# A Mamba, attention and expert kernel on one core: activation table, convolution taps, wide weights and PSUM halves

## The chip, the cores and the metric

The kernel runs on one core of a Trainium2 chip, as a single program. The metric is the device time of one execution in microseconds (us); the number given for a kernel is the median of several executions. Engines are written as in the profile: PE is TensorE (its weight loads PEld), DVE is VectorE, ACT is ScalarE, POOL is GpSimd, SP is the SyncE queue that issues nearly all transfers.

## The reference, cut to what matters

The input x is 4 images of 128 channels and 64 x 64 points, so 4096 tokens each. All is float32.

```python
# layer 0: x + L0(groupnorm(x))
gf   = mamba(tok(x), 2 heads, state 16) + tok(x)          # the "seed": 8 channels
seed = x + detok(gf)
xs   = layernorm(x) split into 8 lanes of 16 channels
ys   = mamba(mamba(xs, state 64), state 64) + xs * skip   # the "cascade", 4 heads, chunks of 64
out  = layernorm(ys + mix(mean(ys))) + seed
h    = dwconv3x3(out @ fc1)                               # 256 channels, 9 taps each
out  = out + gelu(h + dw_b) @ fc2                         # the FFN
# one Mamba: in a chunk of 64, with Acs the running sum of dt * A
Y    = (C @ B^T * tril(exp(Acs_l - Acs_s))) @ x  +  C @ state * exp(Acs)
# layer 1
t = t + softmax(q k^T / sqrt(32)) v @ Wo                  # 4 heads of 32, 4096 keys
t = t + top-2 of 8 experts, weighted by softmax of the router
```

## The kernel before

**Layer 0** works on blocks of 512 tokens (`LB`), eight per image. The list `items` holds 8 seed blocks and 64 cascade blocks (4 images, 8 blocks, 2 Mambas); each goes through four stages, and one step of the loop in `layer0` records the back stage of one item, the front of the next, the preparation of the one after it and the outer part of a fourth, side by side. All these operations go to a recorder, `Deck`. `Deck.flush` then runs a list schedule over them: it has a price for each operation (`price`, with `SIDE` for small matmuls), a rank from the program's order with offsets (`BEHIND`), and rings, which count a tile's buffers. What comes out is one fixed order per engine. It is issued by one line, so in the profile almost all of layer 0 has the line L991, and rows are told apart by their tiles.

The names in `back`: `exponentials` has PE write the exponents ps_d of one pair of chunks (index u, four per block) and ACT take e = exp(ps_d), 128 x 1024. `weigh` multiplies e by the masked products gm on DVE. `within` has PE multiply e with the inputs xp into the PSUM tile py (two banks, 256 columns used of each), and DVE adds its four pieces to y. The items py, e and y above are these.

ACT holds one table of functions at a time. `flush` puts a load of the table with both exponential and logarithm ahead of an exponential or logarithm that follows a SiLU or a GELU; loads for SiLU and GELU, and for whatever else finds its function missing, are put in when the program is compiled.

**The FFN** of an image (`ffn`) runs over its 8 blocks: `merge` (layer norm, seed, residual), `conv` (expand by fc1 to two halves of 128 channels, kept in two fixed tiles h with a halo, then nine taps per half as DVE instructions into acc), `close` (GELU, fc2, residual, store). Three images' FFNs are recorded along with the Mamba steps. The fourth has no Mamba work left beside it: it is recorded into a second flush, with `early`, the first image's projections to q, k and v for the attention (`prepare` in `projections`).

**Layer 1** (`layer1`) is in an order written by hand. A unit is one image, one block of 512 queries and one head: 128 units of 8 groups. A group (`scores`, `context`) has four row-shift matmuls (L1772) and four score matmuls (L1778) into two PSUM tiles ps_s, two exponentials on ACT (L1782) that read them into e, sums of e on POOL (L1784, L1786), four matmuls of e with v (L1799), and four matmuls (L1740) with a DVE maximum each (L1742) for a later unit. L1772 of a group needs the exponentials of the group before to have read its tile. In between, small steps of `prepare` (the next image's projections), `tail` (output projection, router, experts) and `shift` are paid from a budget. Steps with a logarithm are the inverse roots in `rsqrt` (L1029, L1030), the ones in `prepare` (L1480, L1482) and the softmax's denominator in `tail` (L1597, L1598). The layer begins with this line, ahead of the statement that fixes the order of its engines:

```python
        nc.scalar.preload_act_table_set(LNEXP)      # L1577
        ctx.enter_context(tc.manual_schedule(engines={ENG.PE, ENG.DVE, ENG.Pool, ENG.Activation}))
```

Of the kernel before, what the change touches and what calls it, by code (L numbers as in the profile page):

```python
# [31 lines left out]
LB = 512  # L32
# [243 lines left out]
class Mamba:  # L276
# [344 lines left out]
    def back(self, it, out):  # L621
        sh, s, nc = self.sh, self.s, self.sh.nc
        work, const, ng = sh.work, sh.const, s.ng
        y, zs = it["y"], it["zs"]
        y4 = y.rearrange("p (u g c l) -> p u g c l", u=NU, g=ng, c=2)
        es = {}

        def exponentials(u):
            rt = it["rt"]
            ds = [sh.wide("ps_d") for _ in range(2)]  # L630
            for j2 in range(2):
                for g in range(ng):
                    for j in (2 * j2, 2 * j2 + 1):
                        rows = slice(32 * j, 32 * j + 32)
                        dv = ds[j2][:, j % 2, 0:256 * ng].rearrange("s (h g l) -> s h g l", h=4, g=ng)
                        for c in range(2):
                            nc.tensor.matmul(dv[:, :, g, :], lhsT=sh.lt[rows, g, u, Q * c:Q * c + 128],
                                             rhs=rt[rows, :, u, c, :], start=c == 0, stop=c == 1)
            es[u] = []
            for k in range(2):  # L640
                e = work.tile([128, 2, 4, ng * Q], F32, tag="e", bufs=E_BUFS, name="e")
                nc.scalar.activation(e.rearrange("s j h x -> s j (h x)"), ds[k][:, :, 0:256 * ng], AF.Exp)
                es[u].append(e)

        def weigh(u):
            U, i = divmod(u, 2)
            for k, e in enumerate(es[u]):
                for jj in range(2):

                    nc.vector.scalar_tensor_tensor(  # L650
                        e[:, jj], e[:, jj], 1.0,
                        it["gm"][U][:, 2 * i + k, jj:jj + 1, :].to_broadcast([128, 4, ng * Q]), ALU.min, ALU.mult)

        def within(u):
            U, i = divmod(u, 2)
            py = sh.psy.tile([128, 2, LB], F32, tag="y", name="py")
            pyv = py[:, :, 0:128 * ng].rearrange("p c (h x) -> p c h x", h=2)
            for k, e in enumerate(es.pop(u)):
                for g in range(ng):
                    for f in range(2):  # L660
                        for jj in range(2):
                            j = 2 * k + jj
                            for c in range(2):
                                rows = slice(64 * c, 64 * c + 64)
                                nc.tensor.matmul(pyv[32 * j:32 * j + 32, c, :, Q * g:Q * g + Q],
                                                 lhsT=it["xp"][U][rows, g, 4 * i + j, 16 * f:16 * f + 32],
                                                 rhs=e[rows, jj, 2 * f:2 * f + 2, Q * g:Q * g + Q],
                                                 start=f == 0, stop=f == 1)
            for f, name in enumerate(("even", "odd")):
                for c in range(2):  # L670
                    nc.vector.scalar_tensor_tensor(y4[:, u, :, c, :], pyv[:, c, f, :].rearrange("p (g l) -> p g l", g=ng),
                                                   const(name), y4[:, u, :, c, :], ALU.mult, ALU.add)

        exponentials(0)
        yield
        exponentials(1)
        weigh(0)
        yield
        for u in range(NU):
            within(u)  # L680
            if u + 1 < NU:
                weigh(u + 1)
            if u + 2 < NU:
                exponentials(u + 2)
            yield


        nc.gpsimd.tensor_mul(zs, y, zs)
        yield
        yield  # L690
        nc.scalar.activation(y, zs, AF.Square)
        yield

        def by_token(t):
            return t.rearrange("p (u g c l) -> p g c u l", u=NU, g=ng, c=2)

        def product(name, lhsT, rhs):
            p = sh.ps(name)
            for g in range(ng):
                nc.tensor.matmul(p.rearrange("p (c u l) -> p c u l", c=2, l=Q), lhsT=lhsT[:, g, :], rhs=rhs[:, g],  # L700
                                 start=g == 0, stop=g == ng - 1)
            return p

        pm = product("ps_ms", self.ms, by_token(y))
        r = y[:, 0:LB]
        nc.scalar.activation(r, pm, AF.Ln, bias=sh.eps, scale=4.0 / s.nh)
        yield
        nc.scalar.activation(r, r, AF.Exp, scale=-0.5)
        yield
        yield  # L710
        out(product("ps_out", self.wo, by_token(zs)), r)
        yield
# [35 lines left out]
class Op:  # L748
# [3 lines left out]
    def __init__(self, engine):  # L752
        self.engine, self.calls, self.cost, self.deps, self.users = engine, [], 0.0, set(), []
        self.ready, self.rank, self.uses, self.set, self.phase = 0.0, 0.0, set(), None, None
        self.out = self.src = None
        self.both = False
# [4 lines left out]
SIDE = {"py": 0.030, "ps_yo": 0.0215, "ps_d": 0.07}  # L761


class Deck:


    def __init__(self, nc):
        self.nc, self.ops, self.seen, self.rings, self.ring_of = nc, [], {}, {}, {}
        self.phase, self.stage, self.held = None, None, set()
        self.make, self.made, self.count = {}, {}, 0  # L770
# [27 lines left out]
    def record(self, engine, name, args, kw):  # L798
# [4 lines left out]
        src = ins[-1].tensor.name if engine == "tensor" and ins else None  # L803
        op = self.ops[-1] if self.ops else None
        gelu = AF.Gelu_apprx_tanh in args
        if not (op is not None and op.engine == engine and (
                engine == "tensor" and op.out == out.tensor.name and op.src == src or gelu and op.set == GELU)):
            op = Op(engine)
            op.out, op.src = out.tensor.name, src
# [5 lines left out]
        for kind, ap in aps:  # L815
# [10 lines left out]
            if tile in self.ring_of:  # L826
                op.uses.add(tile)
# [3 lines left out]
    def price(self, engine, name, args, kw, out, ins, op):  # L831
# [4 lines left out]
        if engine == "tensor":  # L836
            tile = out.tensor.name.rsplit("_", 1)[0]
# [25 lines left out]
        return 0.15 + (0.00052 if quick else 0.00104) * (free(ins[0]) if name == "tensor_reduce" else n)  # L863
# [12 lines left out]
    def flush(self, tc):  # L876
# [16 lines left out]
        for i, op in enumerate(ops):  # L893
            op.rank = -i - self.BEHIND.get((op.stage, op.engine), 0)
        room, head = dict(self.rings), {}
        phases, whole = {}, {}
        for op in ops:
            if op.set == SILU:
                phases[op.phase] = phases.get(op.phase, 0) + 1
                whole.setdefault(op.phase, set()).update({op.out} & op.uses)  # L900
# [9 lines left out]
        while events:  # L910
# [16 lines left out]
            for e in engines:  # L927
# [3 lines left out]
                while ready[e]:  # L931
# [8 lines left out]
                    for t in whole[op.phase] - opening if op.set == SILU and lock is None else opens:  # L940
# [22 lines left out]
                for t in op.uses - opening:  # L963
# [21 lines left out]
        for i in order:  # L985
# [4 lines left out]
            for name, args, kw in op.calls:  # L990
                getattr(getattr(self.nc, op.engine), name)(  # L991
                    *[self.real(a) for a in args], **{k: self.real(a) for k, a in kw.items()})
        self.ops, self.seen = [], {}
# [12 lines left out]
class Ring:  # L1006
# [5 lines left out]
    def tile(self, shape, dtype, tag=None, bufs=None, name=None):  # L1012
# [10 lines left out]
        return t.ap()  # L1023

# [56 lines left out]
def layer0(tc, T, td, const, ident, eps, where, batches, qkv):  # L1081
# [9 lines left out]
    with ExitStack() as ctx:  # L1091
# [60 lines left out]
        sh.psy = ring(scan, "psy", 1, space=PSUM)  # L1152
        gfd = dram.tile([128, L], F32, name="gfd")

        def load(b, k):
# [128 lines left out]
        def ffn(b):  # L1284

            outs, accs = {}, {}
# [12 lines left out]
            def merge(k):  # L1299

                y = work.tile([128, LB], F32, tag="outs", bufs=3, name="outs")
# [12 lines left out]
                xg = load(b, k)  # L1314
# [13 lines left out]
            def conv(k):  # L1328

                w1 = P("fc1").rearrange("p (g o) -> p g o", g=2)  # L1330
                accs[k] = []
                for g in range(2):
# [18 lines left out]
                    acc = work.tile([128, LB], F32, tag="acc", name="acc")  # L1351
                    a3 = acc.rearrange("p (r w) -> p r w", w=IMG)
                    for i in range(9):
                        tap = h[:, i // 3:i // 3 + 8, i % 3:i % 3 + IMG]
                        w = P("dw")[:, 9 * g + i:9 * g + i + 1]
                        if i == 0:
                            nc.vector.tensor_scalar(a3, tap, w, P("dw_b")[:, g:g + 1], ALU.mult, ALU.add)
                        else:
                            nc.vector.scalar_tensor_tensor(a3, tap, w, a3, ALU.mult, ALU.add)
# [4 lines left out]
            def close(k):  # L1364

                acc = accs.pop(k)
                for a in acc:
                    nc.scalar.activation(a, a, AF.Gelu_apprx_tanh)
                nc.scalar.preload_act_table_set(LNEXP)
                xin = load(b, k)  # L1370
# [11 lines left out]
            for k in range(NBLK + 2):  # L1382
                if k < NBLK:
                    yield from merge(k)
                if k > 1:
# [14 lines left out]
        for s in range(-2, len(items) + 1):  # L1400
# [12 lines left out]
            if 0 < s and items[s - 1].last:  # L1413
                if pending is not None:
                    run((pending, FFN))
                pending = deck.staged("ffn", ffn(items[s - 1].b))
        deck.flush(tc)
        scan.close()
        pw, pp = ring(ctx, "first", 2), ring(ctx, "psf", 4, space=PSUM)
# [3 lines left out]
                              lambda name: pp.tile([128, LB], F32, tag="m", name=name), qkv)  # L1423
# [9 lines left out]
        run((pending, FFN), (early(), 5 * NBLK + 7))  # L1433
# [20 lines left out]
def projections(nc, td, const, eps, P, work, ps, qkv):  # L1454
# [9 lines left out]
    def prepare(b, k):  # L1464
# [19 lines left out]
        nc.gpsimd.tensor_mul(xl, xl, r)  # L1484
# [4 lines left out]
        nc.gpsimd.tensor_mul(v, v, f)  # L1489
        yield 0.4, False  # L1490
        rsqrt(nc, v, v, eps6)
        nc.gpsimd.tensor_add(tk, tk, xl)
        nc.sync.dma_start(out=td[b, :, blk(k)], in_=tk)
        yield 0.4, False
        nc.gpsimd.tensor_mul(v, v, xl)
# [3 lines left out]
        def lower(f, hi, dst):  # L1499
            lo = tmp("lo", "lo", 2, F32R)  # L1500
            nc.gpsimd.tensor_sub(lo, f, hi.bitcast(F32))
# [34 lines left out]
def layer1(tc, T, td, const, ident, eps, where, out, batches, qkv):  # L1536
# [15 lines left out]
    with ExitStack() as ctx:  # L1552
# [27 lines left out]
        prepare = projections(nc, td, const, eps, P, work, ps, qkv)  # L1580
# [355 lines left out]
```

## Time and profile before

| what | value |
|---|---|
| median of 3 executions | 8652.13 us (8643.69 to 8671.25) |
| profiled execution | 8631.42 us, span 8629.6 us |
| granted PE clock, mean | 0.952 |
| busy, share of the span | PE 90%, DVE 74%, ACT 62%, POOL 56% |
| Mamba layer, 100 to 3600 us | PE 3011, DVE 2655, ACT 2499, POOL 466 us busy |
| last FFN with early projections, 3600 to 3860 us | PE 143, DVE 187, ACT 115, POOL 84 us busy |
| attention and experts, 3910 to 8570 us | PE 4498, DVE 3449, ACT 2732, POOL 4248 us busy |

A row of the groups gives line, engine, operation, tiles (out<-in), shapes and count, then the busy time and the mean duration in ns of one instruction, then the engine's idle time just before them with what ended it. A row of the waits gives who waited for whom: total us, times, longest. A row of a timeline gives start, duration, engine, line, operation and tiles, with the idle time before it in brackets. PEclk is the share of its full clock that PE was granted. An fp32 matmul appears as two records.

### The profile page before, as it was taken

The page shows a single profiled execution, that of the slowest core. Times are in us where ns is not written, and L with a number is a line of the kernel's source. Part 1 is how long each engine was busy: PE and PEld are TensorE (multiplying, and loading weights), DVE is VectorE, ACT ScalarE, POOL GpSimd, SP SyncE. Part 2 cuts the span into 40 slices and gives each one's busy share as a digit, 9 for nine tenths or more (in the row PEclk, how much of TensorE's full clock was granted, in tenths as well). Part 3 has the DMA queues.
Part 4 walks back from the last instruction along what each step waited for, and adds up shares of the span by engine and source line. Part 5 has one row for each costly group of instructions (what it writes and reads, how often), then busy time and mean ns, then how long its engine had stood idle before and what let it go on. Part 6 is the DMA issues. An engine that isn't in the chain of part 4 may idle for free.

```text
span 8629.6 us, 191814 instructions
## 1 busy us (share of the span) xinstructions
PE 7746.4 (90%) x80156; PEld 4572.8 (53%) x80156; DVE 6391.4 (74%) x11795; ACT 5390.8 (62%) x6666; POOL 4824.7 (56%) x3273
## 2 busy tenths in 40 slices
PE   5888888888888888759999999999999999999998
PEld 3566666666666666424454545545444545455544
DVE  5767677877887787767777777777777777777775
ACT  5776677777777677535656556565556565555554
POOL 1111111111111111138999899998889998999997
PEclk9999999999999999869999999999999999999999
DMA  4211211211112111135444445444444544444442
GB/s 136 88 45 46 56 40 47 60 51 50 52 55 59 54 52 46 50 107 131 121 127 116 127 112 135 120 122 123 121 117 123 128 120 127 115 113 118 120 117 61
DMA packets 306609, 800.58 MB, mean 93 GB/s; under 512 B 43984, under 2 KB 61008, under 8 KB 288848
## 3 DMA queue, kind: packets, MB, share of 16 engines
q1 hardware_dynamic: 304848, 780.94, 34.3%
q8 instruction: 633, 10.37, 0.5%
q10 hardware_dynamic: 432, 5.12, 0.2%
q14 instruction: 232, 1.90, 0.1%
q0 software_dynamic: 464, 2.25, 0.1%
HBM read 595.19 MB, written 192.94 MB: 91 GB/s over the span
## 4 chain that ended last, share of the span: by engine, by line
PE 39%; POOL 14%; ACT 6%; DVE 5%; issue 3%; DMA 1%; SPq 0%; POOLq 0%; ACTq 0%; DVEq 0%
POOL s L1784 9%; PE ps_mx L1740 8%; PE acc L1799 7%; PE ps_s L1778 6%; POOL es L1786 4%; PE ps_s L1772 3%; ACT e L1782 2%; PE ps_den L1812 2%; PE ps_e L1688 2%; PE py L991 1%; DVE mx L1742 1%; DVE acc L991 1%; PE ps_d L991 1%; PE ps_ms L991 1%; PE ps_x L991 1%
## 5 line engine op out<-in xcount | busy, mean ns | idle before, releaser
L1742 DVE TENSOR_REDUCE mx<-ps_mx 128x1 f32<-128x512 f32 x4096 | 2791.9, 689 | 951.7 <-PE ps_mx L1740 944.1
L1782 ACT ACTIVATE e<-ps_s 128x1024 f32<-128x1024 f32 x2048 | 1985.3, 1021 | 1633.2 <-PE ps_s L1778 1533.9
L1784 POOL TENSOR_TENSOR s<-e 128x1024 f32<-128x1024 f32 x1024 | 2441.5, 2384 | 338.2 <-ACT e L1782 334.6
L1740 PE MATMUL ps_mx<-k,q 128*128 128x512 f32 x4096 | 1892.6, 472 | 63.9 <-DVE mx L1742 29.7
L1786 POOL TENSOR_TENSOR es<-s 128x512 f32<-128x512 f32 x1024 | 1311.7, 1281 | 80.3
L1778 PE MATMUL ps_s<-q,k 128*128 128x512 f32 x4096 | 1291.4, 397 | 0.0
L1799 PE MATMUL acc<-e,V 128*32 128x512 f32 x8192 | 1100.1, 609 | 0.0
L1740 PEld LDWEIGHTS ps_mx<-k,q 128*128 128x128 f32 x4096 | 780.4, 191 | 545.0 <-DVE mx L1742 215.9
L1778 PEld LDWEIGHTS ps_s<-q,k 128*128 128x128 f32 x4096 | 779.2, 190 | 138.6 <-issue 2.9
L991 DVE SCALAR_TENSOR_TENSOR e<-e,gm 128x512 f32<-128x512 f32 (+1 forms) x1152 | 718.4, 666 | 82.4 <-ACT e L991 82.2
L1772 PEld LDWEIGHTS ps_s<-mr,ones 32*128 32x128 f32 x4096 | 215.2, 182 | 990.8 <-ACT e L1782 587.6
L991 DVE SCALAR_TENSOR_TENSOR y<-py,const,y 128x128 f32<-128x128 f32 (+1 forms) x1152 | 367.8, 339 | 462.5 <-PE py L991 461.4
L1772 PE MATMUL ps_s<-mr,ones 32*128 32x512 f32 x4096 | 571.8, 497 | 92.2 <-ACT e L1782 91.2
L991 ACT ACTIVATE e<-ps_d 128x1024 f32<-128x1024 f32 (+1 forms) x576 | 550.5, 976 | 165.8 <-PE ps_d L991 151.5
L991 PE MATMUL py<-e,xp 64*32 64x128 f32 x17408 | 518.0, 276 | 44.7 <-DVE y L991 43.8
L991 POOL TENSOR_TENSOR zs<-y,zs 128x1024 f32<-128x1024 f32 (+1 forms) x72 | 173.7, 2412 | 563.5 <-DVE y L991 563.0
L991 POOL TENSOR_TENSOR u<-acs 128x512 f32<-128x512 f32 x72 | 76.1, 1057 | 737.5 <-DVE acs L991 643.5
L991 PEld LDWEIGHTS py<-e,xp 64*32 64x32 f32 x17408 | 400.5, 107 | 139.5 <-issue 66.6
L991 PE MATMUL ps_d<-rt,lt 32*128 32x256 f32 x4352 | 374.2, 309 | 29.3 <-ACT e L991 13.0
L991 DVE SCALAR_TENSOR_TENSOR acc<-h,pb,acc 128x512 f32<-128x512 f32 x512 | 385.6, 787 | 3.8
L991 POOL CAST x<-halo_casc 128x8 fp32r<-128x8 f32 x64 | 18.6, 291 | 636.0 <-PE ps_C L991 635.9
L991 PEld LDWEIGHTS ps_d<-rt,lt 32*128 32x128 f32 x4352 | 270.3, 188 | 186.3 <-issue 72.2
(351 smaller groups left out, 12266.3 us busy)
## 6 DMA issues: line engine op xcount, KB each, us to landing
k<-kd SPq DMA_DIRECT2D x512, 512.0 KB, 6.3
x<-hl SPq DMA_DIRECT2D x256, 256.0 KB, 5.2
V<-vd SPq DMA_DIRECT2D x128, 512.0 KB, 10.2
cd<-raw SPq DMA_DIRECT2D x256, 256.0 KB, 5.1
parts<-cd SPq DMA_DIRECT2D x128, 512.0 KB, 6.1
xin<-in_x SPq DMA_DIRECT2D x128, 256.0 KB, 3.1
q<-qd SPq DMA_DIRECT2D x512, 64.0 KB, 4.7
hl<-hi SPq DMA_DIRECT2D x72, 256.0 KB, 2.0
```

The costliest lines, as they stand in the source:

```text
L991: getattr(getattr(self.nc, op.engine), name)(*[self.real(a) for a in args], **{k: self.real(a) for k, a in kw.items()})
L1688: nc.tensor.matmul(pe, lhsT=xl[:, tok], rhs=ew[:, e:e + 2, :].rearrange("p e c -> p (e c)"), start=True, stop=True)
L1740: nc.tensor.matmul(p, lhsT=q4s[u][:, 128 * qt:128 * qt + 128], rhs=k4s[u][:, blk(kb)], start=True, stop=True)
L1742: nc.vector.tensor_reduce(mxs[u][:, qt, kb:kb + 1], p, AX.X, ALU.max)
L1772: nc.tensor.matmul(pts[j // 2][:, j % 2, :], lhsT=ones2[rows, :], rhs=mrows[u][rows, :], start=True, stop=False)
L1778: nc.tensor.matmul(pts[j // 2][:, j % 2, :], lhsT=k4s[u][:, 128 * kt:128 * kt + 128], rhs=q4s[u], start=False, stop=True)
L1782: nc.scalar.activation(e[:, 2 * j:2 * j + 2], pts[j], AF.Exp)
L1784: nc.gpsimd.tensor_add(s2, e[:, 0:2], e[:, 2:4])
L1786: nc.gpsimd.tensor_add(s, s2[:, 0], s2[:, 1])
L1799: nc.tensor.matmul(accs[u][32 * j:32 * j + 32, :], lhsT=Vs[u][:, 4 * g + j, :], rhs=e[:, j, :], start=g == 0, stop=g == 7)
L1812: nc.tensor.matmul(p[32 * j:32 * j + 32, :], lhsT=ones, rhs=s, start=True, stop=True)
```

## The change

1. `Deck.flush` ends with a load of the exponential-and-logarithm table if the last table used was another one.
2. `ffn` takes its pools as arguments. Its loop expands both halves of a block before it closes the block two before. For the last image it gets pools of its own with one more buffer for outs and acc, four PSUM buffers of its own and two more, and the first four taps of each half become matmuls with diagonal weights that add up in PSUM (`diagonal`); DVE does the other five. The tap's bias moves into the GELU for all images. The early projections use DVE instead of POOL for their elementwise products, the old two PSUM buffers, and a stage name of their own in the planner.
3. e has its axes in another order, so that one DVE instruction of 1024 elements per partition weighs what two of 512 did.
4. py becomes two fixed banks (`Halves`), each used in two halves by turns; the planner is told of two buffers.
5. The planner's prices change: ps_yo, ps_d, and 0.05 more for a scalar_tensor_tensor. Its sets become dicts.

```diff
@@ Mamba.back
-                e = work.tile([128, 2, 4, ng * Q], F32, tag="e", bufs=E_BUFS, name="e")
-                nc.scalar.activation(e.rearrange("s j h x -> s j (h x)"), ds[k][:, :, 0:256 * ng], AF.Exp)
+                e = work.tile([128, 4, 2, ng * Q], F32, tag="e", bufs=E_BUFS, name="e")
+                nc.scalar.activation(e.rearrange("s h j x -> s j h x"),
+                                     ds[k][:, :, 0:256 * ng].rearrange("s j (h x) -> s j h x", h=4), AF.Exp)
...
-                for jj in range(2):
-
-                    nc.vector.scalar_tensor_tensor(
-                        e[:, jj], e[:, jj], 1.0,
-                        it["gm"][U][:, 2 * i + k, jj:jj + 1, :].to_broadcast([128, 4, ng * Q]), ALU.min, ALU.mult)
+                e2 = e.rearrange("s h j x -> s h (j x)")
+                gm = it["gm"][U][:, 2 * i + k].rearrange("s j x -> s (j x)")
+                nc.vector.scalar_tensor_tensor(e2, e2, 1.0, gm[:, None, :].to_broadcast([128, 4, 2 * ng * Q]),
+                                               ALU.min, ALU.mult)
...
-            py = sh.psy.tile([128, 2, LB], F32, tag="y", name="py")
-            pyv = py[:, :, 0:128 * ng].rearrange("p c (h x) -> p c h x", h=2)
+            pyv = [t[:, 0:128 * ng].rearrange("p (h x) -> p h x", h=2) for t in sh.psy.tiles("py")]
@@ planner
-SIDE = {"py": 0.030, "ps_yo": 0.0215, "ps_d": 0.07}
+SIDE = {"py": 0.030, "ps_yo": 0.0185, "ps_d": 0.08}
...
-        return 0.15 + (0.00052 if quick else 0.00104) * (free(ins[0]) if name == "tensor_reduce" else n)
+        return (0.2 if name == "scalar_tensor_tensor" else 0.15) + (0.00052 if quick else 0.00104) * (free(ins[0]) if name == "tensor_reduce" else n)
@@ Deck.flush, behind the loop that issues the order
+        if table not in (None, EXPS):
+            self.nc.scalar.preload_act_table_set(LNEXP)
@@ new
+class Halves:
+    def __init__(self, deck, pool):
+        self.deck, self.turn = deck, 0
+        self.banks = [pool.tile([128, LB], F32, tag=f"bank{c}", name=f"bank{c}") for c in range(2)]
+    def tiles(self, name):
+        deck, at = self.deck, LB // 2 * (self.turn % 2)
+        self.turn += 1
...
+            deck.rings.setdefault((id(self), c), 2)
+            tiles.append(t.ap()[:, at:at + LB // 2])
+        return tiles
@@ layer0
-        sh.psy = ring(scan, "psy", 1, space=PSUM)
+        sh.psy = Halves(deck, scan.enter_context(tc.tile_pool(name="psy", bufs=1, space=PSUM)))
...
-        def ffn(b):
+        def ffn(b, work, ps, depth=0, diag=0, taps=None, ps_taps=None):
...
-                y = work.tile([128, LB], F32, tag="outs", bufs=3, name="outs")
+                y = work.tile([128, LB], F32, tag="outs", bufs=3 + depth, name="outs")
...
+            def diagonal(k):
+                made[k] = [rows(ps_taps("ps_taps")) for _ in range(2)]
+                for g in range(2):
+                    for i in range(diag):
+                        nc.tensor.matmul(made[k][g], lhsT=taps[:, g, i, :], rhs=tap(g, i), start=i == 0,
+                                         stop=i == diag - 1)
...
-                    for i in range(9):
...
+                    for i in range(diag, 9):
...
+                            nc.vector.scalar_tensor_tensor(rows(acc), tap(g, i), w, sums, ALU.mult, ALU.add)
+                        sums = rows(acc)
...
-                    nc.scalar.activation(a, a, AF.Gelu_apprx_tanh)
+                    nc.scalar.activation(a, a, AF.Gelu_apprx_tanh, bias=P("dw_b")[:, g:g + 1])
...
+                if 0 < k <= NBLK:
+                    yield from expand(k - 1)
+                    if diag:
+                        diagonal(k - 1)
                 if k > 1:
                     yield from close(k - 2)
...
-        run((pending, FFN), (early(), 5 * NBLK + 7))
+        pending = deck.staged("ffn", ffn(pending, last, single("f", 4), 1, 4, taps, single("t", 2)))
+        run((pending, FFN), (deck.staged("early", early()), 5 * NBLK + 7))
@@ projections (and the four other lines like it; pairs is nc.vector for the early ones, nc.gpsimd in layer 1)
-        nc.gpsimd.tensor_mul(xl, xl, r)
+        pairs.tensor_mul(xl, xl, r)
```

## The prediction, made before the changed kernel ran

> **What bounds the kernel now.** I read the page's slices first, to cut the span into stages.
>
> ```profile
> PE   5888888888888888759999999999999999999998
> ...
> ACT  5776677777777677535656556565556565555554
> POOL 1111111111111111138999899998889998999997
> PEclk9999999999999999869999999999999999999999
> ```
>
> A slice is 216 us. PE leads in slices 2 to 16 (the Mamba layer), nothing leads in 17 and 18 (the last FFN, at a lowered clock), and PE with POOL leads from 19 on (attention). The table of windows gives the sums:
>
> ```profile
> core 0: us, PE busy (x) PEld busy (x) DVE busy (x) ACT busy (x) POOL busy (x), PEclk, DMA share, GB/s
> 100.00:3600.00 3500.00, 3011.45 (x54117) 2130.58 (x54115) 2655.19 (x5030) 2498.52 (x3298) 465.70 (x533) 0.93 0.19 54
> 3600.00:3860.00 260.00, 143.12 (x308) 58.48 (x308) 186.63 (x237) 114.75 (x192) 83.66 (x66) 0.69 0.28 92
> 3910.00:8570.00 4660.00, 4498.02 (x25367) 2334.35 (x25365) 3448.89 (x6269) 2731.73 (x3107) 4247.91 (x2627) 0.99 0.47 120
> ```
>
> Attention: PE 97%, POOL 91%, ACT only 59%. By these sums ACT could lose work for nothing. So I asked the timeline of ACT what it does between two exponentials, and the table of waits from 3950 us on who waits for it:
>
> ```profile
> 5122.86 1.94 ACT L1782 ACTIVATE e<-ps_s 128x1024 f32<-128x1024 f32 x2 [2.80 <-PE ps_s L1778]
> 5124.81 1.28 ACT L1597 ACT_TABLE_LOAD   x1
> 5126.11 0.63 ACT L1597 ACTIVATE cx<-parts 128x512 f32<-128x512 f32 x1
> 5126.76 1.28 ACT L1598 ACT_TABLE_LOAD   x1
> 5128.05 0.63 ACT L1598 ACTIVATE cx<-cx 128x512 f32<-128x512 f32 x1
> 5128.59 1.92 ACT L1782 ACTIVATE e<-ps_s 128x1024 f32<-128x1024 f32 x2
> ```
> ```profile
> ACT e L1782 <- PE ps_s L1778: 1518.2, 884, 7.2
> ...
> PEld ps_s L1772 <- ACT e L1782: 578.7, 637, 5.3
> ...
> PE ps_s L1772 <- ACT e L1782: 87.5, 132, 4.4
> ```
>
> A logarithm loads one table, the exponential behind it another. ACT mostly waits for PE, but at these places it turns round: PE stands 87.5 us before L1772, its score buffers not yet read by e. The page's busy PE hides part of such stalls, since ends of matmuls are modelled.
>
> In the Mamba layer PE is busy 86%, DVE 76%, ACT 71%, each waiting for the others in turn. The rows that the change touches, and two of the waits there:
>
> ```profile
> L991 DVE SCALAR_TENSOR_TENSOR e<-e,gm 128x512 f32<-128x512 f32 x1024 | 671.4, 697 | 53.1 <-ACT e L991 52.9
> L991 DVE SCALAR_TENSOR_TENSOR y<-xs,wc_casc,y 128x1024 f32<-128x1024 f32 x64 | 81.8, 1279 | 0.6
> ```
> ```profile
> DVE y L991 <- PE py L991: 456.9, 230, 11.0
> ...
> PE py L991 <- DVE y L991: 36.8, 38, 1.9
> ```
>
> And in the last FFN, where the chain of waits has DVE acc as its largest part (27.8%):
>
> ```profile
> L991 DVE SCALAR_TENSOR_TENSOR acc<-h,pb,acc 128x512 f32<-128x512 f32 x140 | 116.1, 881 | 0.9
> ...
> L991 PE MATMUL ps_var<-ln_r,const_sb 128*128 128x512 f32 x16 | 14.5, 1007 | 44.0 <-ACT ln_r L991 44.0
> ...
> L991 POOL TENSOR_TENSOR xl<-xl,r 128x512 f32<-128x512 f32 x8 | 12.3, 1542 | 34.3 <-ACT r L991 34.3
> ```
>
> **Part 1, the table at the layer's end.** Attention has its own preload (L1577), but the trace has it at 0.7 us, as ACT's first load: it was moved to the head of the program, and the GELU set of the last FFN is in force when attention starts. From there the trace has 224 loads of 1283 ns (56 + 56 at L1029/L1030, 32 + 32 at L1597/L1598, 24 + 24 at L1480/L1482), 287 us of ACT. In the built order of the changed kernel a load stands behind the last FFN's last ACT work, and none after it; all else in attention has the same order on all five engines. So 224 loads go. How much of the 287 us is on PE's path? Three readings. (a) Only the idle put down to e: 87.5 us. (b) Starts of the first e of each of the 1024 groups: without a load in the period the mean is 4.34 us (916), with loads 6.38 us (107): 107 x 2.04 = 218 us. That is too much: periods with loads also hold the Ln, the Exp and often a variance matmul, and the period behind one is short (3.62 us, PE catching up). (c) PE's own starts. L1772 starts 0.52 us behind the matmul before it, and its third matmul 0.003 us behind its second, in at least half of all groups. Summed over what exceeds this, the 191 groups with a load in the 5.5 us before lose 63 + 82 = 145 us, the 833 others 5 us. I take (c), -145, and keep -88 and -218 as ends. Late next is POOL (91% busy; at 145 us less, 4248 of 4515, 94%), which still fits. The queue of ACT loses instructions only; nothing is put behind a new wait.
>
> The Trainium skill, page "ScalarE: Activation LUTs", section "What ACT_TABLE_LOAD costs", counts 1283 ns for the load and some 1380 ns of drain with it. Here the load agrees, but no drain is to be seen: the load starts 0.01 us after e ends, and Ln 0.02 us after the load. By the page the 224 loads would be an estimated 596 us; the sum goes by the rows.
>
> **Part 2, the Mamba layer.** *Weights 1024 wide*: for the 64 cascade items 1024 instructions of 697 ns become 512. The nearest row of that width is y<-xs, 1279 ns: 714 - 655 = 59 us less on DVE. The 128 seed instructions (256 wide, 420 ns) become 64 of some 700 ns, about 9 us less. DVE is not the busiest here, so between 0 and 68 us reach the end. *PSUM halves*: py used 256 columns of each of two banks, once; now two halves of the same two banks take turns, to spare PE the 36.8 us before py. But the built order shows what the waits became. They go by the bank, not by the half: 266 of VectorE's waits for py name matmuls of the *next* pair of tiles in the other half, and py waits for a y addition at 258 places instead of 75. Behind such a wait on VectorE stand the next weighing and the softplus steps, and py and the state matmuls wait for those; behind one on PE stands all of the next item's projection. Price of one: where py waited for y it was 36.8/75 = 0.49 us a place, so 183 more places on PE are up to 90 us lost; VectorE's have idle time to hide in. *New prices in the planner* (ps_d, ps_yo, one more 0.05 us for a scalar_tensor_tensor) and the FFN's two expansions put ahead of the closing reorder all engines; ACT gets 5 loads more (6 us). Reordering has no row; I give it no sign. Ends: -59 - 37 = -96, and +90. I take -20: a third of the DVE gain, nothing for the halves.
>
> The Trainium skill, page "PSUM — Partial Sum Buffer", section "PSUM bank collisions raise a hardware error", says to guard PSUM by bank and quadrant, not by address; that speaks against halves as a second buffer. No row of before shows it, since py was never written and read in the same stretch; by the page the 37 us don't come.
>
> **Part 3, the last FFN (3600 to 3860 us, 260 us).** Off DVE: four of nine taps, 64 x 881 ns = 56 us. On DVE, from POOL: six products of each of 8 early projections, 48 x 0.69 (row of a 512-wide tensor_tensor, 684 to 689 ns) = 33 us. The taps left should drop from 881 to the 751 ns that this row has in the Mamba layer, where POOL is idle: 80 x 0.13 = 10 us. Other DVE rows with two SBUF inputs (outs, 1188 and 977 ns) lose some 6 us. DVE: 187 - 56 + 33 - 10 - 6 = 148 us. PE gains 64 fp32 matmuls of 128x512, each two records; ps_var takes 1007 ns a record at this stage's clock of 0.69 (2.0 us), and 656 ns in attention at 0.99 (36.6/32 = 1.14 us): +73 to +129 us on 143. At the low clock PE would need 272 us, at the full one some 100 + 73 = 173. So PE becomes the busiest. It can't be both dense and cold throughout; with 85% of density this is 204 to 320 us: ends -56 and +60. The added wait: the fifth tap, now first on DVE, waits for the four diagonal matmuls (4 to 8 us after h); behind it on DVE stand the next block's merge and the early projections. Block-deep buffers (outs 4, acc 3, PSUM 4 + 2) are meant to cover that; without the cover it is 16 x 4 = 64 us, which is the same upper end. I take 245 us: -15. GELU's bias operand is 16 x 0.06 = 1 us of ACT (686 ns with a bias at h, 623 without), behind PE; eight small DVE instructions for the diagonals are under 5 us, beside the first loads.
>
> **Sum.** -145 - 20 - 15 = -180 against the profiled execution's 8631.4: 8451. The three timed runs have their median 20.7 above that execution, so 8472.
>
> **Rivals.** *Much was hidden*: only reading (a) comes off attention and PE waits for POOL or DVE instead: -88 - 20 - 15 gives 8529, and with a cold last FFN (+60) 8604. For it: PE is 97% busy there. Against: of the 150 us of late starts, 145 lie behind a load. *The Mamba layer gains too*: all of DVE's 59 and PE's 37, and the dense FFN: -145 - 96 - 56 gives 8355. For it: in long stretches DVE runs without a gap. Against: the bank-wide waits. *The halves interlock* (slower): 266 + 183 = 449 new cross waits, each like the mean stall of those 38 that stalled, 36.8/38 = 0.97 us, all on the path: +435 - 160 gives 8927. It turns the sign once a new wait costs 160/449 = 0.36 us on average. Against: half of the old places didn't stall at all, and VectorE is free a quarter of the time. *Loads stay*: the built order has none, so I give it nothing.
>
> **How the numbers follow.** Forecast 0.60, hidden 0.20, Mamba gains 0.14, interlock 0.06. The root of the squared ends is 113 us down (73, 76, 41) and 145 up (57, 110, 75): 8359 to 8617; the hidden case lies inside, 8355 just outside, so I say 8350 to 8600. A change under 0.3% (26 us) can't be told from none. Faster: 0.60 + 0.14 + 0.18; same 0.03 (0.02 of hidden, 0.01 of interlock); slower the other 0.05.
>
> **What would show it.** Right: no ACT_TABLE_LOAD past the first microseconds of attention, e's mean period there near 4.4 us, L1772's place in the waits for e nearly gone; e<-e,gm at 1024 wide near 1.28 us; 64 pairs of records ps_taps, and PE's clock above 0.8 in the last FFN. Wrong: attention's stretch shorter by under 90 us, with POOL named before e; or the Mamba layer longer by over 50 us, with py<-y and y<-py grown.

## The result, and the profile after

The changed kernel takes 8557.53 us (median of 4, 8550.11 to 8571.92) where the kernel before, with one more run, takes 8651.68 us: a ratio of 0.989, 95% interval 0.9868 to 0.9912. It is 94 us faster; 180 were forecast. The profiled execution has 8550.11 us, span 8548.1.

The slices of the page of the changed kernel, in three of the rows shown of the kernel before:

```profile
PE   5888888888888888888999999999999999999998
...
POOL 1111110111111111105999999999999999999997
PEclk8989999999989998998999999999999999999999
```

The dip that PE and its clock had in slices 17 and 18 is gone, and POOL starts its dense stretch no earlier although the last FFN is shorter: something ahead of it grew. The windows, asked by the changed kernel's own stages:

```profile
core 0: us, PE busy (x) PEld busy (x) DVE busy (x) ACT busy (x) POOL busy (x), PEclk, DMA share, GB/s
100.00:3600.00 3500.00, 3035.47 (x52433) 2149.48 (x52433) 2530.70 (x4316) 2443.03 (x3223) 472.40 (x521) 0.92 0.19 53
...
3709.00:3900.00 191.00, 161.50 (x436) 73.50 (x435) 153.21 (x227) 122.86 (x195) 14.62 (x15) 0.93 0.38 124
...
3951.00:8490.00 4539.00, 4436.57 (x25373) 2312.40 (x25371) 3453.33 (x6270) 2450.45 (x2888) 4245.86 (x2627) 0.99 0.48 123
```

In the first window ACT and DVE got less done (3223 instructions and 4316, 3298 and 5030 before; of DVE's some are one for two now). Three marks, each the start of an instruction, split the span: the last ps_out (the last Mamba item's output), the first e and the last e of the attention.

| stretch | before | after | difference |
|---|---|---|---|
| start to last ps_out (Mamba layer) | 3601.5 us | 3710.2 us | +109 us |
| to first e (last FFN, first loads) | 307.5 us | 241.4 us | -66 us |
| first to last e (attention) | 4659.0 us | 4535.5 us | -124 us |
| rest | 61.5 us | 60.9 us | -1 us |

The differences add up to -81 us, that of the two profiled executions; the medians are 94 us apart.

**Attention.** In the kernel before, the load of L1577 runs as ACT's first instruction and not where attention begins:

```profile
0.74 1.28 ACT L1577 ACT_TABLE_LOAD   x1 [0.74 <-PEq L1928]
```

ACT's timeline of the changed kernel around a softmax denominator, and the waits from 3950 us on:

```profile
4272.67 1.94 ACT L1848 ACTIVATE e<-ps_s 128x1024 f32<-128x1024 f32 x2 [2.80 <-PE ps_s L1844]
4274.49 0.63 ACT L1663 ACTIVATE cx<-parts 128x512 f32<-128x512 f32 x1
4275.15 0.63 ACT L1664 ACTIVATE cx<-cx 128x512 f32<-128x512 f32 x1
4276.52 1.94 ACT L1848 ACTIVATE e<-ps_s 128x1024 f32<-128x1024 f32 x2 [0.73 <-PE ps_s L1844]
```
```profile
ACT e L1848 <- PE ps_s L1844: 1594.0, 945, 9.2
...
PEld ps_s L1838 <- ACT e L1848: 418.7, 488, 2.0
...
ACT e L1848 <- POOL es L1852: 81.2, 22, 4.8
...
PE ps_s L1838 <- ACT e L1848: 20.4, 43, 1.1
```

No load stands between the exponentials: the next e comes 3.85 us after the one before (5.73 in the lines of before), and it waits for PE, not PE for it. PE's idle time before the row-shift matmuls fell from 87.5 to 20.4 us.

**The Mamba layer.** The waits from 100 to 3600 us of the changed kernel, where py's tiles are named bank:

```profile
DVE y L996 <- PE bank L996: 574.5, 307, 10.4
...
PE ps_st L996 <- DVE gm L996: 98.5, 41, 4.6
...
PE bank L996 <- DVE y L996: 21.7, 45, 1.9
```

In the same window the kernel before has:

```profile
DVE y L991 <- PE py L991: 461.4, 234, 11.0
...
PE py L991 <- DVE y L991: 43.8, 41, 3.1
...
PE ps_st L991 <- DVE gm L991: 38.0, 32, 3.4
```

PE stands idle for y less, as the halves were to bring about. But DVE stands 113 us longer in front of y, and PE 60 us longer for the masked products gm before it can form the states ps_st (ps_g, which gm reads, and ps_st share two PSUM buffers).

What DVE waits for can be counted, since each of the 288 pairs has a known number of matmuls. In the changed kernel 207 y additions, with 172 us of idle time before them, start over 0.25 us after the last matmul of their own pair has ended: they wait for matmuls of the next pair. In the kernel before there is none. How far this makes gm late is shown in part. At nearly all the places where PE waits for gm, DVE had stood idle for y after gm's input was ready, but that idle time covers at most 41 of the 99 us (16 of 38 before). In the rest, gm stood behind other work in DVE's order.

**The last FFN.** The groups from 3710 to 3900 us:

```profile
L996 DVE SCALAR_TENSOR_TENSOR acc<-h,pb,acc 128x512 f32<-128x512 f32 x78 | 61.9, 806 | 1.7
L996 PE MATMUL ps_taps<-h,taps 128*128 128x512 f32 x128 | 57.7, 595 | 0.9 <-ACT h L996 0.9
...
L996 DVE SCALAR_TENSOR_TENSOR acc<-h,pb,ps_taps 128x512 f32<-128x512 f32 x16 | 12.0, 747 | 9.7 <-PE ps_taps L996 8.0 <-PE ps_f L996 1.7
```

The 64 tap matmuls cost PE 57.7 us, 595 ns a record, at a granted clock of 0.93; DVE waits 8.0 us for them in all.

### The profile page after: what moved, and what is told of

It reads as the page before. It is cut to its first block, busy times and chain, and to the rows that moved or that the text cites. A ratio compares the mean times of both kernels' runs of the same rounds, so it can differ in the third digit from the quotient of the medians.

```text
span 8548.1 us, 191291 instructions
## 1 busy us (share of the span) xinstructions
PE 7815.6 (91%) x80284; PEld 4646.5 (54%) x80284; DVE 6321.3 (74%) x11211; ACT 5117.9 (60%) x6448; POOL 4775.4 (56%) x3225
## 4 chain that ended last, share of the span: by engine, by line
PE 30%; POOL 20%; issue 3%; DVE 3%; ACT 1%; DMA 0%; POOLq 0%; DVEq 0%; SPq 0%; ACTq 0%
POOL s L1850 12%; PE ps_mx L1806 7%; PE acc L1865 6%; PE ps_s L1844 6%; POOL es L1852 5%; PE ps_s L1838 3%; PE ps_e L1754 2%; PE ps_den L1878 2%; DVE mx L1808 1%; PE ps_taps L996 1%; POOL parts L1668 0%; PE ps_sh L1825 0%; PE ps_f L1743 0%; POOL cx L1670 0%; PE ps_f L1742 0%
## 5 line engine op out<-in xcount | busy, mean ns | idle before, releaser
L996 DVE SCALAR_TENSOR_TENSOR y<-bank,const,y 128x128 f32<-128x128 f32 (+1 forms) x1152 | 355.3, 338 | 589.0 <-PE bank L996 586.4
L996 DVE SCALAR_TENSOR_TENSOR e<-e,gm 128x1024 f32<-128x1024 f32 (+1 forms) x576 | 656.7, 1161 | 69.3 <-ACT e L996 68.5
L996 PE MATMUL bank<-e,xp 64*32 64x128 f32 x17408 | 592.9, 276 | 36.1 <-DVE y L996 27.0
L1838 PE MATMUL ps_s<-mr,ones 32*128 32x512 f32 x4096 | 532.1, 496 | 20.4 <-ACT e L1848 20.4
L996 PEld LDWEIGHTS bank<-e,xp 64*32 64x32 f32 x17408 | 439.2, 108 | 165.7 <-DVE y L996 58.4
L1865 PEld LDWEIGHTS acc<-e,V 128*32 128x32 f32 x8192 | 161.4, 108 | 364.2 <-issue 358.4
```

Of the source, the lines that this page charges most:

```text
L996: getattr(getattr(self.nc, op.engine), name)(*[self.real(a) for a in args], **{k: self.real(a) for k, a in kw.items()})
L1838: nc.tensor.matmul(pts[j // 2][:, j % 2, :], lhsT=ones2[rows, :], rhs=mrows[u][rows, :], start=True, stop=False)
L1865: nc.tensor.matmul(accs[u][32 * j:32 * j + 32, :], lhsT=Vs[u][:, 4 * g + j, :], rhs=e[:, j, :], start=g == 0, stop=g == 7)
```

## The experiments

The table above gives three questions: are the attention's 124 us the table loads alone; which part of the change cost the Mamba layer 109 us; which shortened the last FFN. All numbers are last ps_out, last ps_out to first e, and first to last e, from the profile of each run. How far a stage moves with nothing changed is seen from the runs themselves: the last ps_out is at 3601.5 and 3633.5 us in two kernels with the same order up to there, and between 3619.6 and 3643.2 us in four others that share one. The runs come from several chips: on those of the experiments the kernel before takes 8665.6 us (e1 to e4, one run), 8656.5 (e5 to e8) and 8644.8 (e9 to e12).

**The table alone** (e1): the kernel before, with the end of `flush` from the change.

```diff
+        if table not in (None, EXPS):
+            self.nc.scalar.preload_act_table_set(LNEXP)
         self.ops, self.seen = [], {}
```

> The kernel before with one addition: the table load at the end of the recorded layer. If the attention's gain is the table loads alone, attention (first to last e) goes from 4658 us to the 4535 us of the changed kernel, within 10 us, and the Mamba layer (last ps_out at 3600 us) and the last FFN stay as they were: total near 8631 - 123 = 8508 us. Rival: part of the 123 us comes from elsewhere (what stands in which buffer when attention starts): then attention stays above 4560 us.

Measured: 8532.34 us (one run); attention 4524.0 us, no load in it, last ps_out 3633.5 us, last FFN 312.1 us. The two added lines give the whole of the attention's gain, 135 us here, and in this run the kernel is faster than the full change. The rival falls. The total is 24 us above the expected 8508 because the last ps_out came 32 us later than before, with the same order up to there.

**The Mamba layer: three undos.** Each takes one part out of the changed kernel: e2 the halves, e3 the wide weighing, e4 the new prices.

```diff
# e2
-        sh.psy = Halves(deck, scan.enter_context(tc.tile_pool(name="psy", bufs=1, space=PSUM)))
+        sh.psy = ring(scan, "psy", 1, space=PSUM)
...
+            py = sh.psy.tile([128, 2, LB], F32, tag="y", name="py")
+            pyv = [py[:, c, 0:128 * ng].rearrange("p (h x) -> p h x", h=2) for c in range(2)]
# e3: e as [128, 2, 4, ng * Q], weighed by two instructions, rhs=e[rows, jj, 2 * f:2 * f + 2, ...]
# e4
+SIDE = {"py": 0.030, "ps_yo": 0.0215, "ps_d": 0.07}
+        return 0.15 + (0.00052 if quick else 0.00104) * (free(ins[0]) if name == "tensor_reduce" else n)
```

> The changed kernel with py as before: one tile of two banks, one buffer, the planner told of one. Theory A (the halves' bank-wide waits cost the Mamba layer its 109 us): the last ps_out comes back from 3709 us to 3600 us or earlier, total near 8440 us. Theory B (the new prices and the order they make cost it): the last ps_out stays above 3680 us, total above 8520 us. Theory C (1024-wide weighing makes py wait for a whole e): also above 3680 us.

> The changed kernel with the weighing as before: two instructions of 512 for each e, the old order of e's axes. Theory C (the wide weighing costs the Mamba layer its time): the last ps_out comes back from 3709 us to near 3600 us. Theories A and B: it stays, or goes up by up to 59 us, the DVE time that the wide form saves: 3700 to 3770 us.

> The changed kernel with the planner's old prices (ps_yo 0.0215, ps_d 0.07, no extra 0.05 for a scalar_tensor_tensor). Theory B (the prices cost the Mamba layer its time): the last ps_out comes back from 3709 us to near 3600 us. Theories A and C: it stays between 3680 and 3740 us.

Measured: last ps_out at 3674.8 us without the halves, 3796.9 without the wide weighing, 3725.9 with the old prices (8491.89, 8625.89 and 8548.77 us in all, one run each). Of the theories only A moves the right way, and by 35 us, a third of what it claimed and little more than the scatter; in this combination the wide weighing helps by more than its DVE time. No single undo gives the 109 us back, so I ran the other corners.

**The other four combinations.** e5 has all three undone; e6, e7 and e8 put one part back.

> The changed kernel with halves, wide weighing and prices all undone; the table load, the new last FFN and the new order inside the earlier three FFNs stay. If the single undos add up (halves +34, wide -88, prices -17 in the last ps_out), the last ps_out is at 3709 - 34 + 88 + 17 = 3780 us and the earlier FFNs' order would have to cost some 150 us. If instead the three interact through the planned order, and the FFNs' order costs nothing, the last ps_out is at 3600 to 3640 us, as in the kernel before and in the kernel with the table alone, and the total near 8631 - 124 - 66 = 8440 to 8475 us.

> As the kernel with halves, weighing and prices undone, but with the wide weighing. If its DVE saving reaches the end, the last ps_out is 20 to 60 us earlier than there; if effects add up as in the single undos, 88 us earlier; if the order decides by chance, anywhere within 60 us on either side.

> As the kernel with halves, weighing and prices undone, but with the new prices. If the prices make a worse order, the last ps_out is over 30 us later than there; if effects add up, 17 us earlier.

> As the kernel with halves, weighing and prices undone, but with the halves. If the bank-wide waits cost time whatever the order, the last ps_out is over 30 us later than there (34 us if effects add up), with DVE's waits for the two banks above those for py; if two halves free PE as meant, it is earlier, by up to 37 us.

Measured, in one table with the earlier ones (last ps_out in us, and from 100 to 3600 us the wait of DVE's y for py):

| weighing, prices | without halves | with halves | cost of the halves |
|---|---|---|---|
| narrow, old | e5: 3662.2, 497 us | e8: 3772.2, 577 us | +110 us |
| wide, old | e6: 3694.5, 378 us | e4: 3725.9, 538 us | +31 us |
| narrow, new | e7: 3749.7, 504 us | e3: 3796.9, 606 us | +47 us |
| wide, new | e2: 3674.8, 437 us | after: 3710.2, 575 us | +35 us |

e5 fits neither of its expectations: it lies 118 us below the sum of the undos and 22 us above the range for no effect of the FFNs' order. The halves cost time in all four rows, 56 us on average, and DVE's wait for py grows by 81 to 160 us in each. The wide weighing has no sign of its own: +32 without halves and with old prices, -75, -46 and -87 elsewhere. Nor have the prices: +88, -20, +25, -16. So effects don't add up; the order that the planner makes of them decides.

Single differences of some 30 us are no more than the stage moves by itself; that all four have one sign, and the waits with them, speaks for the halves as a loss. The sign also holds with each total taken as a share of the kernel before on its own chip: +119, +14, +34 and +79 us. Idle time of y additions whose own pair was done, counted as above, is 149, 151, 172 and 172 us with halves and nothing in the four kernels without; PE's wait for gm grows in each row too, from 38.4 to 82.1, 12.6 to 73.1, 73.2 to 116.3 and 30.3 to 98.5 us. Open is how much of the loss is the waits and how much the other order, since with the halves the planner is also told of two buffers; the two weren't taken apart.

The waits of e8, and of e5, which differs from it by the halves alone:

```profile
DVE y L995 <- PE bank L995: 577.4, 306, 11.3
...
PE ps_st L995 <- DVE gm L995: 82.1, 51, 4.3
PE bank L995 <- DVE y L995: 23.8, 63, 0.9
```
```profile
DVE y L996 <- PE py L996: 496.7, 239, 11.1
...
PE py L996 <- DVE y L996: 47.6, 43, 2.4
...
PE ps_st L996 <- DVE gm L996: 38.4, 36, 3.4
```

With halves PE's matmuls stand for y at more places (63, not 43) but half as long in all, the y additions stand 81 us longer for PE, and PE 44 us longer for gm. e5, with the Mamba parts undone, was timed: 8478.35 us (median of 4), ratio 0.9793 (0.9777 to 0.981).

**The earlier FFNs' order** (e9): as e5, with the first three images' FFNs expanding each half directly before its taps again.

```diff
+                    if not depth:
+                        yield from expand(k, (g,))
...
-                if 0 < k <= NBLK:
+                if depth and 0 < k <= NBLK:
                     yield from expand(k - 1)
```

> As the kernel with halves, wide weighing and prices undone, and in the first three FFNs also the old order (a half is expanded directly before its taps). Left of the change: the table load, the new last FFN, the bias in the GELU. If the FFNs' order cost the rest, the last ps_out goes from 3661 us back to 3600 to 3635 us and the total to 8420 to 8450 us; if it is scatter between chips, it stays above 3645 us and the total near 8478 us.

Measured: 8463.89 us (median of 5), ratio 0.9794 (0.978 to 0.9808); last ps_out 3619.6 us. The ratio is that of e5. The mark is 43 us earlier than e5's, but the other three kernels with this order have up to 3643.2, and e5's profiled execution was 17 us above its median. So it stays open whether this order costs anything. Either kernel beats both of the given ones.

**The last FFN**, from e9: e10 takes the taps off PE, e11 gives the early products back to POOL, e12 takes the additional buffers away. The expectation of e12 speaks of the old order of expansions too, but the kernel that ran keeps the new one: with taps on PE, `expand` still comes ahead of `close`.

```diff
# e10
-        pending = deck.staged("ffn", ffn(pending, last, single("f", 4), 1, 4, taps, single("t", 2)))
+        pending = deck.staged("ffn", ffn(pending, last, single("f", 4), 1))
# e11
-                              ps, qkv, nc.vector)
+                              ps, qkv, nc.gpsimd)
# e12
-                    if not depth:
+                    if not diag:
...
-                if depth and 0 < k <= NBLK:
+                if diag and 0 < k <= NBLK:
...
+        pending = deck.staged("ffn", ffn(pending, last, single("f", 2), 0, 4, taps, single("t", 2)))
```

> As the kernel with the old order in the first three FFNs, but with all nine taps of the last FFN on DVE; its buffers and the early projections on DVE stay. If the taps on PE made the last FFN 66 us shorter (last ps_out to first e: 308 us before, 243 us now), it goes back to 290 us or more: 64 taps of 0.75 us are 48 us more for DVE, which has some 200 busy in 245. If the buffers did it, it stays under 265 us.

> As the kernel with the old order in the first three FFNs, but with the early projections' products on POOL again. Theory: DVE loses 33 us of its own but its remaining 80 taps go from some 0.76 to 0.88 us again (10 us), so last ps_out to first e is 5 to 20 us shorter than 243 us, or the same if PE sets the pace by now. Rival: POOL's slower products (1.47 us) lengthen the chain to q, k and v: 5 to 20 us longer.

> As the kernel with the old order in the first three FFNs, but the last FFN with the old number of buffers (outs 3, acc 2, two PSUM buffers) and the old order of its expansions; taps on PE and early projections on DVE stay. If buffers and order let the blocks overlap, last ps_out to first e goes from 243 to 265 us or more; if the taps on PE alone did it, it stays within 10 us.

Measured, last ps_out to first e: e9 240.3 us, e10 270.3, e11 247.9, e12 278.5. The nine kernels with the changed last FFN, the Mamba variants and e9 included, lie between 238.4 and 246.9, so e10 and e12 stand clear of them and e11, 1 us above, doesn't. e10 falls between its two expectations, e12 meets the one for the buffers. The taps are worth 30 us and the buffers 38 us, neither the 66 alone. What the new order of the last FFN's expansions is worth no run shows. What the taps do is seen in the window from the last ps_out to 52 us before the first e, of e9 and of e10:

```profile
3619.60:3807.90 188.30, 159.41 (x431) 72.66 (x430) 148.87 (x222) 120.14 (x193) 14.11 (x14) 0.93 0.38 124
```
```profile
3643.20:3861.50 218.30, 135.18 (x304) 56.92 (x302) 188.21 (x287) 116.85 (x189) 14.52 (x14) 0.76 0.34 112
```

With the taps PE has 57 us of matmuls more (128 records of 595 ns, overlapping) but only 24 us more busy time: its clock is granted at 0.93, not 0.76, and its other matmuls are shorter (ps_h 626 ns a record, not 724). In e12 a group of the same stretch tells what the buffers are for. DVE's first tap writes acc, of which there are two, one for each half; it waits until fc2's matmul (ps_f) of the block before has read the one that it takes, and starts 0.04 us after that matmul:

```profile
L996 DVE SCALAR_TENSOR_TENSOR acc<-h,pb,ps_taps 128x512 f32<-128x512 f32 x16 | 11.9, 746 | 32.3 <-PE ps_f L996 31.4 <-PE ps_taps L996 0.9
```

Who wins in e11 is inside the scatter. Its taps took 946 ns against 769 in e9, with POOL busy 41% of the stretch instead of 7%; slower taps were expected:

```profile
L996 DVE SCALAR_TENSOR_TENSOR acc<-h,pb,acc 128x512 f32<-128x512 f32 x74 | 69.4, 946 | 5.5 <-ACT h L996 3.5
```

## Why the prediction was right in sign and half in size

The time lies in the stated range and on the forecast side, but two of the three terms of the sum lay outside their ends and partly cancelled. That it lies in the range is luck in part: without the last FFN's 51 us more than forecast it would be near 8609, above the range. Of the prediction's signs of being wrong, one came: the Mamba layer longer by over 50 us, with DVE's wait for py grown, though PE's wait for y shrank.

- **Part 1, the table: right.** -145 was forecast by reading (c), PE's late starts; -124 came in the changed kernel and -132 to -142 in the twelve experiments. Reading (a), idle time alone, and reading (b), periods, would have given -88 and -218. The late starts of L1772 fell from 150 to 37 us; 29 of these 37 us lie within 5.5 us behind a Ln or its Exp, which stay. POOL did not become the bound: e's waits for es, POOL's sums, rose only from 62 to 81 us. The 224 loads of 1283 ns were worth some 0.6 us each on the path. The Trainium skill, page "ScalarE: Activation LUTs", section "What ACT_TABLE_LOAD costs", adds a drain to each load; it was visible in no run, where the next instruction of ACT starts 0.01 us behind a load (median).
- **Part 2, the Mamba layer: the step that failed.** -20 with ends -96 and +90 was forecast, +109 came. The built order had shown the cross waits, and I priced those on PE (183 places, up to 90 us) and let VectorE's hide in its idle time. It was the other way round: PE's waits for y fell from 43.8 to 21.7 us, and the y additions, held up at the next pair's matmuls for 172 us, delayed gm and, in part by that, PE's state matmuls. An engine that is idle a quarter of the time can still be late with what the bound engine needs next. Of the 109 us the halves make 35 in this combination (up to 110 in others), and up to 32 may be scatter, since the same order had its last ps_out at 3601.5 and 3633.5 us. The rest is put down, by elimination, to the order made by prices, weighing and FFNs, to which I gave no sign; its cause stays open. The range of that order should have been some 90 us wide to either side, as the 88 us between e5 and e7 and the -87 between e3 and the changed kernel show. The wide weighing's instruction was sized well: 1221 ns in the same window, against the 1279 taken.
- **The interlock rival** named the mechanism, at 0.06, with a price of 0.97 us for each of 449 waits and a turning point of 0.36. Measured it is 35/449 = 0.08 us in the changed kernel, and 110/449 = 0.24 us in e8 if that order has as many.
- **The rule of guarding by bank** (the Trainium skill, page "PSUM — Partial Sum Buffer", section "PSUM bank collisions raise a hardware error"), which spoke against halves, was the better guide: no combination gained from them. What the chip does without such waits no run here shows; a kernel whose waits go by the half wasn't tried.
- **Part 3, the last FFN: a term mis-sized.** -15 with ends -56 and +60 was forecast, -66 came. DVE's sum was right (148 us forecast, 153 in the 191 us window). PE's was not: +73 to +129 us forecast for the taps, 57.7 measured, since 656 ns a record was taken as the least and 595 came, and records of matmuls that follow each other overlap: 0.90 us a matmul, not the 1.14 taken. That they go into one PSUM tile need not be why a record is shorter; another row of ps_var in the attention before, L1477, has 592 ns. And the stage's low clock was carried over although the added work itself raised it. The added wait for the diagonal matmuls, bounded at 64 us, is 8.0 us. The taps left on DVE fell from 881 to 806 ns, not to 751 as in the Mamba layer before, where POOL was busy 13% of the time and not idle.

## What to carry to other kernels

Look for the table loads in the trace of a stage that should need one set, and at where in the trace a preload really runs: here one statement stood at the head of its stage and ran at 0.7 us. Before a PSUM bank is split into halves to serve as two buffers, look in the built order at what the waits are kept by; if it is the bank, the halves add waits, here on VectorE above all. When an order comes out of a list schedule, undo the parts one by one and in combination before any is called good: two of three parts here changed sign with the others.

## What the runs showed of the hardware that I had not expected

More matmuls made a stage's other matmuls faster: with 57 us of taps added, PE's granted clock in the last FFN rose from 0.76 (e10) to 0.93 (e9) and its busy time by only 24 us. A record of an fp32 matmul of 128x512 took 595 ns there (ps_taps, clock 0.93); for ps_var it took 1007 ns in the last FFN before (0.69), and 592 and 656 ns in the attention before (0.99).
